# Weight parts made two units ahead, in pieces: a four-layer network on one core

## The chip, the cores and the metric

One core of a Trainium2 chip runs the whole network in one launch. The metric is the device time of that launch in microseconds (us). The five engines of the core run on their own and meet at semaphores: TensorE (PE, matrix products into PSUM), VectorE (DVE), ScalarE (ACT), GpSimd (POOL) and SyncE (SP, which here only issues DMA).

## The reference, cut to what matters

Three of the four layers are of this kind; the input is 4 x 32 x 32 x 16, and each layer is added to its input after a group norm (8 groups of 2 channels, over a whole image):

```python
first   = einsum('ijyx,byxc->bijc', M, inputs)
kern    = G as (h*w*f) filters of 3 x 3 x c          # one filter for each (i, j, f)
shifted = conv(inputs, kern)                         # b, (h w f), y, x
diff    = relu(inputs[:, None, None] - shifted)
second  = einsum('ijyx,bijyxc->bijc', W, diff)
out     = first - second
```

For each of the 1024 x 16 filters a full 32 x 32 image is made, clamped, weighted and summed to one number per batch. The third layer is another thing: running maxima and minima over intervals, then two steps of `max over k of sigmoid(ft[i, k] + rt[k, j] + b)`.

The convolution's 144 taps and channels are the contraction. The kernel takes `relu(x - s)` as `-min(s - x, 0)` by taking 1 off the filter's middle tap (`pick`), and keeps near float32 accuracy by splitting weights and input into an upper part (12 mantissa bits masked off) and the rest, and summing products of the parts.

## The kernel before

The work is cut into 6 phases (3 convolution layers, 2 halves of the batch), 8 tiles of 128 filters' places, and 32 steps per tile: 16 output channels `f` times 2 batches `b`. That makes 1536 steps. Four `f` are a unit: 192 units of eight steps, and each unit's weights are loaded and made ready once.

A unit's weights come as `raw` (slots 0, 1: the first 128 rows; slot 2: the last 16 rows repeated). `prep` takes the picked 1 off slot 1. `prep_rest` makes the four parts that the matmuls read:

```python
    RAWS = 3
    ...
    def prep(u, at=0, to=FU, eng=nc.gpsimd):
        ...
        eng.tensor_tensor(raws[u][:, 1, at:to], raws[u][:, 1, at:to], pick[...], ALU.subtract)   # L174

    def prep_rest(u, at=0, to=FU, eng=nc.gpsimd):
        ...
        high = upper(w8, f"w{u}{at}")                                  # VectorE, L164
        nc.scalar.activation(WD, high, AF.Copy, scale=-EPS)            # ScalarE, L197
        halve(W9, w9, low_w)                                           # ScalarE, L142
        eng.tensor_copy(WU, high)                                      # GpSimd,  L199
        eng.tensor_tensor(WL, w8, high, ALU.subtract)                  # GpSimd,  L200
        for r in (slice(32, 64), slice(96, 128)):
            eng.tensor_tensor(W9[r], W9.bitcast(F32)[r], w9[r], ALU.add)      # GpSimd, L202
        eng.tensor_tensor(WD, WD.bitcast(F32), WL.bitcast(F32), ALU.add)      # GpSimd, L203
```

Each of the parts has two buffers (`wpool`, bufs=2). A step has two halves, and the second half of one step is issued behind the first half of the next:

```python
    def first_part(step):
        ps = bank_pair(...)                       # one of 4 pairs of PSUM banks
        products(ps, WU x iy (2 slots), WL x iz (2 slots))             # TensorE, 8 matmuls
        nc.scalar.activation(ps, ps, AF.Copy, scale=1.0 + EPS)         # ScalarE, L531
        return ps

    def second_part(step, ps):
        products(ps, WD x iyz (2 slots), W9 x im9)                     # TensorE, 6 matmuls
        nc.vector.scalar_tensor_tensor(junk, ps, 0.0, chunks[n], op0=ALU.min, op1=ALU.mult,
                                       accum_out=accs[...])            # VectorE, L545

    def conv_layer(phase, behind):
        for t in range(NT):
            ...
            for at, (f, b) in enumerate(steps):
                u = n * NU + f // FU
                if at % (FU * GB) == 1:           # once per unit
                    prep_rest(u + 1)
                    prep(u + 2)
                    load_raw(u + 3)
                if at == 4:
                    load_chunk(n + 1)
                step = (phase, t, f, b)
                open_steps.append((step, first_part(step)))
                if len(open_steps) > 1:
                    second_part(*open_steps.pop(0))
                wait -= 1
                if wait <= 0:
                    wait = next(behind, 1 << 20)  # a piece of the next phase's work
```

`behind` is a generator. It gives out the work that the next phase needs (group norm, the input written to DRAM and read back shifted, its split into `iy`, `iz`, `iyz`, the interval layer, the products with `M`) piece by piece; `yield 5` means that five steps pass until the next piece. Two parts of it matter here:

```python
    def group_norm(g, name, dst):
        part = sums(X[g], ...)                        # VectorE
        yield 2
        m = mean_of(part, ...)                        # GpSimd partition_all_reduce, L240
        yield 5
        ... mean, xc                                  # VectorE
        yield 1
        ... squares, part                             # VectorE
        yield 2
        v = mean_of(part, ...)                        # GpSimd partition_all_reduce, L240
        yield 5
        nc.scalar.activation(rstd, v, AF.Sqrt, ...)   # ScalarE
        yield 2
        ...
    def before_conv(g, layer):
        yield from group_norm(...)
        nc.vector.transpose(xt[g]..., xn)
        ... write xt to DRAM (xs), four DMA on the ScalarE and SyncE queues
        yield 2
        ... read it back as 9 shifted copies (raw), 24 DMA on the ScalarE and SyncE queues
        yield 9
        for b in range(GB):
            split(nc.gpsimd, g, b, ...)
            yield 3
        ...
```

The interval layer holds its tables in a buffer of 8192 float32 per partition (`tables`), which is the buffer of the `M` matrix at other times (tag `big`), and has two further buffers for the sums (`dp`).

At the start, the input of batch 0 is normalized on ScalarE and VectorE, and that of batch 1 on GpSimd, behind the first step.

Of the kernel before, what the change touches and what calls it, by code (L numbers as in the profile page):

```python
# [8 lines left out]
F32 = mybir.dt.float32  # L9
F32R = mybir.dt.float32r  # L10
I32 = mybir.dt.int32
AF = mybir.ActivationFunctionType
ALU = mybir.AluOpType
AX = mybir.AxisListType

P = 128
B, H, C = 4, 32, 16
NG = 2
GB = B // NG
GC = GB * C  # L20
# [9 lines left out]
FU = 4  # L30
# [4 lines left out]
T1 = H + 1  # L35
# [5 lines left out]
def net_kernel(ctx: ExitStack, tc: tile.TileContext, x, xq, xi, convs, iv_w, iv_b, out):  # L41
# [19 lines left out]
    nc = tc.nc  # L61
# [3 lines left out]
    wpool = ctx.enter_context(tc.tile_pool(name="wpool", bufs=2))  # L65
    work = ctx.enter_context(tc.tile_pool(name="work", bufs=1))
    ivp = ctx.enter_context(tc.tile_pool(name="ivp", bufs=1))
# [16 lines left out]
    nc.sync.dma_start(XQ, xq)  # L84


    RAWS = 3
    raws, units, chunks = {}, {}, {}

    def load_raw(u):  # L90
        if u < n_chunks * NU:
            n = u // NU
            raws[u] = wpool.tile([P, 3, FU, P], F32, tag="raw", bufs=RAWS, name=f"raw_{u}")
            nc.sync.dma_start(raws[u], convs[phases[n // NT][1]][2][n % NT, u % NU])
# [18 lines left out]
    F0 = 2  # L113
    raws[0] = wpool.tile([P, 3, FU, P], F32, tag="raw", bufs=RAWS, name="raw_0")
    nc.scalar.dma_start(raws[0][:, :, :F0], convs[0][2][0, 0][:, :, :F0])
# [25 lines left out]
    def halve(dst, src, mask):  # L141
        nc.scalar.activation(dst, src, AF.Copy, scale=mask[:, 1:2])  # L142
# [16 lines left out]
    def upper(src, name):  # L159

        t = work.tile([P, 2, PITCH], F32, tag="upper", bufs=2, name=f"upper_{name}")
        t = t.rearrange("p s n -> p (s n)")[:, : src.shape[1] * src.shape[2]]
        t = t.rearrange("p (s n) -> p s n", s=src.shape[1])
        nc.vector.tensor_scalar(  # L164
            t.bitcast(I32), src.bitcast(I32), HIGH, None, op0=ALU.bitwise_and
        )
        return t

    def prep(u, at=0, to=FU, eng=nc.gpsimd):

        if u >= n_chunks * NU:
            return
        f0 = u % NU * FU
        eng.tensor_tensor(  # L174
            raws[u][:, 1, at:to], raws[u][:, 1, at:to],
            pick[:, f0 + at : f0 + to].unsqueeze(2).to_broadcast([P, to - at, P]),
            ALU.subtract,
        )

    def prep_rest(u, at=0, to=FU, eng=nc.gpsimd):  # L180

        if u >= n_chunks * NU:
            return
        if at == 0:
            units[u] = [
                wpool.tile([P, 2, FU, P], F32R, tag=tag, name=f"{tag}_{u}")
                for tag in ("WU", "WL", "WD")
            ] + [wpool.tile([P, FU, P], F32R, tag="W9", name=f"W9_{u}")]
        src = raws[u]
        if to == FU:  # L190
            del raws[u]
        w8 = src[:, :2, at:to].rearrange("p s f k -> p s (f k)")
        w9 = src[:, 2, at:to]
        WU, WL, WD = (t[:, :, at:to].rearrange("p s f k -> p s (f k)") for t in units[u][:3])
        W9 = units[u][3][:, at:to]
        high = upper(w8, f"w{u}{at}")
        nc.scalar.activation(WD, high, AF.Copy, scale=-EPS)  # L197
        halve(W9, w9, low_w)
        eng.tensor_copy(WU, high)  # L199
        eng.tensor_tensor(WL, w8, high, ALU.subtract)  # L200
        for r in (slice(32, 64), slice(96, 128)):
            eng.tensor_tensor(W9[r], W9.bitcast(F32)[r], w9[r], ALU.add)  # L202
        eng.tensor_tensor(WD, WD.bitcast(F32), WL.bitcast(F32), ALU.add)  # L203

    def split(eng, g, b, name):

        high = upper(raw[:, :2, b], f"x{name}{b}")
        eng.tensor_copy(iy[g][:, :, b], high)
        eng.tensor_tensor(iz[g][:, :, b], raw[:, :2, b], high, ALU.subtract)

    def scale_low(g, b):
        z = iz[g][:, :, b]
        nc.scalar.activation(z, z.bitcast(F32), AF.Copy, scale=1.0 / EPS)  # L213

    def difference(eng, g, b):
        eng.tensor_tensor(  # L216
            iyz[g][:, :, b], iy[g].bitcast(F32)[:, :, b], iz[g].bitcast(F32)[:, :, b], ALU.subtract
        )
# [152 lines left out]
    def interval_layer(g):  # L371

        R = 2 * GC
# [4 lines left out]
        tables = big.tile([P, 8192], F32, tag="big", name=f"tables_{g}")  # L378
        n = (H + M) * (M + H)
# [19 lines left out]
        k = 0  # L399
# [10 lines left out]
            )  # L410
            yield 2

        r = tables[: R + GC, 2 * n : 2 * n + T1 * T1].rearrange("p (i j) -> p i j", j=T1)
        nc.gpsimd.memset(r[:R], 0.0)
        nc.gpsimd.affine_select(
            out=r[:R, :H, 1:], in_=pp[k][:, :H, M:], pattern=upper, compare_op=ALU.is_ge, fill=0.0,
# [35 lines left out]
        def step(name, ftp, rt, bias):  # L452

            ft = ivp.tile([P, QI, T1], F32, tag="ft", name=f"ft_{name}{g}")
            nc.scalar.copy(ft, ftp)  # L455
            yield 2
            s = ivp.tile([P, QI, T1], F32, tag="s", name=f"s_{name}{g}")
            last = None
            for i in range(QI + 1):
                if i < QI:  # L460
                    t = ivp.tile([P, T1, T1], F32, tag="dp", bufs=2, name=f"dp_{name}{g}{i}")
                    nc.gpsimd.tensor_tensor(  # L462
                        t,
                        ft[:, i, :].unsqueeze(1).to_broadcast([P, T1, T1]),
                        rt,
                        ALU.add,
                    )
                if last is not None:
                    nc.vector.tensor_reduce(s[:, i - 1, :], last, axis=AX.X, op=ALU.max)
                last = t  # L470
                yield 6
            for q in range(NQ):
                o = slice(GC * q, GC * (q + 1))
                nc.scalar.activation(
                    r[R:, QI * q : QI * (q + 1), :], s[o], AF.Sigmoid, bias=bias[o]
                )
            yield 2
# [82 lines left out]
    def conv_layer(phase, behind):  # L560


        wait = 0
        accs[phase] = work.tile([P, NT, GC], F32, tag="acc", bufs=2, name=f"acc_{phase}")
        for t in range(NT):
            n = phase * NT + t
            steps = [(f, b) for f in range(C) for b in range(GB)]
            if n == 0:
                steps.sort(key=lambda s: (s[0] // FU, s[1]))
            for at, (f, b) in enumerate(steps):  # L570
                u = n * NU + f // FU
                if at % (FU * GB) == 1:
                    prep_rest(u + 1)
                    prep(u + 2)
                    load_raw(u + 3)
                if at == 4:
                    load_chunk(n + 1)
                step = (phase, t, f, b)
# [5 lines that stand above are left out]
                    wait = next(behind, 1 << 20)  # L584
        for _ in behind:
            pass
# [96 lines left out]
    def sides(eng, b, slot):  # L683

        v = raw[:, slot, b].rearrange("p (y x) -> p y x", x=HP)
        if slot == 2:
            eng.memset(v[:, :, H - 1 : H], 0.0)
            eng.memset(v[64:, HI - 1, :H], 0.0)
        for side, at in (
            ("left", v[:, :, 0]), ("right", v[:, :, H - 1]),  # L690
            ("top", v[:, 0, :H]), ("bottom", v[:, HI - 1, :H]),
        ):
            if f"{side}{slot}" in keep:
                eng.tensor_scalar_mul(at, at, keep[f"{side}{slot}"])

    def normal(eng, b, slot):
        v = raw[:, slot, b, :RUN]
        if eng is nc.scalar:
            eng.activation(v, v, AF.Identity, bias=minus_mean0[:, b : b + 1])
            eng.activation(v, v, AF.Copy, scale=rstd0[:, b : b + 1])  # L700
        else:
            eng.tensor_scalar(  # L702
                v, v, mean0[:, b : b + 1], rstd0[:, b : b + 1], op0=ALU.subtract, op1=ALU.mult
            )
# [10 lines left out]
    difference(nc.vector, 0, 0)  # L715
    halve_rest(im9[0][:, 0], raw[:, 2, 0], low_x)
    load_raw(1)
    load_raw(2)
    prep(0, F0, FU, nc.vector)
    prep_rest(0, F0, FU)  # L720
    prep(1)

    def rest_of_start():

        nc.sync.dma_start(X[0], x[0])
        for slot in (0, 1, 2):
            normal(nc.gpsimd, 1, slot)
            sides(nc.gpsimd, 1, slot)
        yield 1
        split(nc.vector, 0, 1, "00")  # L730
        scale_low(0, 1)
        difference(nc.vector, 0, 1)
        yield 1
        halve(im9[0][:, 1], raw[:, 2, 1], low_x)
        halve_rest(im9[0][:, 1], raw[:, 2, 1], low_x)
        nc.gpsimd.memset(zero, 0.0)
        zeros(0)
        xns[0] = work.tile([P, NT, GC], F32, tag="xn", bufs=2, name="xn_00")
        yield from group_norm(0, "c00", xns[0])
# [79 lines left out]
```

## Time and profile before

Two runs took 3530.45 and 3538.63 us, median 3534.54. The profiled execution spans 3538.9 us.

| operation, by line | engine | count | mean of one |
|---|---|---|---|
| matmul 64 x 512 | TensorE | 21504 | 428 to 442 ns, two at a time |
| scaling of PSUM, L531 | ScalarE | 1536 | 1002 ns |
| min, times, sum, L545 | VectorE | 1536 | 1223 ns |
| `WD`, L197 | ScalarE | 193 | 1053 ns |
| `W9` halved, L142 | ScalarE | 193 | 704 ns |
| `upper_w`, L164 | VectorE | 193 | 722 ns |
| `WU`, L199 | GpSimd | 192 | 1038 ns |
| `WL`, L200 | GpSimd | 192 | 2378 ns |
| `W9` sum, L202 | GpSimd | 384 | 1278 ns |
| `WD` sum, L203 | GpSimd | 192 | 2396 ns |
| `prep`, L174 | GpSimd | 191 | 1091 ns |

How to read it: TensorE works through steps in order, and all else is there to keep it fed. The matmuls of two halves of the array run together, so the mean of one is about twice the time between starts. The page lists each group with its busy time and the idle time of its engine just before it, and names who ended that idle time. The chain of waits follows the end of the program back from each instruction to what released it. The 40 slices of the page show TensorE at 7 or 8 tenths nearly everywhere after the start, and the granted clock between 8 and 9 tenths: the time is spread over the whole span, not sitting in one place.

### The profile page before, as it was taken

How to read it: one execution, taken by the hardware profiler on the slowest of the kernel's cores; microseconds unless marked ns; L12 is line 12 of the kernel's file. 1: busy time of each engine (PE TensorE's matmuls, PEld its weight loads, DVE VectorE, ACT ScalarE, POOL GpSimd, SP SyncE). 2: the span in 40 equal slices, each digit the busy share in tenths (PEclk: the TensorE clock that was granted, in tenths of full speed). 3: DMA queues.
4: the chain of work that ended last, by engine and by line, in shares of the span. 5: the costliest groups of instructions: out<-in, count | busy, mean ns of one | idle time of the engine just before them, and what ended most of it. 6: DMA issues, size and time to landing. Idle time of an engine off the chain costs nothing.

```text
span 3538.9 us, 56292 instructions
## 1 busy us (share of the span) xinstructions
PE 2966.8 (84%) x21970; PEld 2346.7 (66%) x21970; DVE 2155.1 (61%) x3519; ACT 1874.1 (53%) x1993; POOL 1983.0 (56%) x1284
## 2 busy tenths in 40 slices
PE   5788888788888778888878888787888878888888
PEld 4566777566676666777656667565676656777767
DVE  5565666566666556666656666666666655656666
ACT  4454555455555545555544555454555554555555
POOL 4564555465555464555556665565666555555554
PEclk8899999899999989999988899898889989999999
DMA  2221111211111131111111111221111122111110
GB/s 89 72 99 49 56 56 51 63 57 51 51 57 60 43 116 46 59 59 51 53 46 52 52 42 51 63 66 42 43 51 51 51 79 90 51 52 57 57 55 11
DMA packets 49514, 203.78 MB, mean 58 GB/s; under 512 B 11872, under 2 KB 13280, under 8 KB 48480
## 3 DMA queue, kind: packets, MB, share of 16 engines
q1 hardware_dynamic: 42688, 195.07, 16.4%
q10 hardware_dynamic: 6432, 5.10, 0.7%
q8 instruction: 173, 2.83, 0.3%
q14 instruction: 93, 0.76, 0.1%
q0 software_dynamic: 128, 0.02, 0.0%
HBM read 199.19 MB, written 0.98 MB: 57 GB/s over the span
## 4 chain that ended last, share of the span: by engine, by line
PE 73%; ACT 9%; issue 6%; POOL 5%; DVE 4%; DMA 2%; ACTq 0%; DVEq 0%; POOLq 0%; SPq 0%
PE pc L510 73%; ACT pc L531 5%; ACT W L142 4%; DVE junk L545 2%; POOL W L202 1%; DMA raw<-xs 1%; POOL WD L203 1%; POOL WL L200 1%; DVE upper_w L164 1%; PE pf L318 1%; POOL raw L174 0%; DMA xs<-xt 0%; POOL tables L384 0%; POOL raw L702 0%; POOL WU L199 0%
## 5 line engine op out<-in xcount | busy, mean ns | idle before, releaser
L545 DVE SCALAR_TENSOR_TENSOR junk<-pc,WT 128x1024 f32<-128x1024 f32 x1536 | 1878.9, 1223 | 1328.8 <-PE pc L510 1284.9
L531 ACT ACTIVATE pc<-pc 128x1024 f32<-128x1024 f32 x1536 | 1527.9, 1002 | 1174.3 <-PE pc L510 1128.0
L510 PE MATMUL pc<-iyz,WD 64*128 64x512 f32 x6144 | 1134.6, 442 | 531.4 <-ACT pc L531 519.1
L510 PEld LDWEIGHTS pc<-iyz,WD 64*128 64x128 f32 x6144 | 657.1, 206 | 755.8 <-ACT pc L531 558.5
L510 PE MATMUL pc<-iy,WU 64*128 64x512 f32 x6144 | 1103.1, 431 | 18.3 <-DVE junk L545 10.0
L510 PE MATMUL pc<-iz,WL 64*128 64x512 f32 x6144 | 1096.2, 428 | 8.5 <-POOL WL L200 7.3
L199 POOL CAST WU<-upper_w 128x1024 fp32r<-128x1024 f32 (+1 forms) x192 | 199.4, 1038 | 1220.5 <-DVE upper_w L164 1183.4
L510 PEld LDWEIGHTS pc<-iy,WU 64*128 64x128 f32 x6144 | 676.9, 205 | 178.1 <-DVE junk L545 14.8
L510 PEld LDWEIGHTS pc<-iz,WL 64*128 64x128 f32 x6144 | 677.0, 203 | 153.8 <-POOL WL L200 9.3
L510 PE MATMUL pc<-im,W 64*128 64x512 f32 x3072 | 695.9, 433 | 0.0
L200 POOL TENSOR_TENSOR WL<-raw,upper_w 128x1024 fp32r<-128x1024 f32 (+1 forms) x192 | 456.6, 2378 | 115.1 <-PE pc L510 57.2
L202 POOL TENSOR_TENSOR W<-W,raw 32x512 fp32r<-32x512 f32 (+1 forms) x384 | 490.8, 1278 | 26.4
L203 POOL TENSOR_TENSOR WD<-WD,WL 128x1024 fp32r<-128x1024 f32 (+1 forms) x192 | 460.0, 2396 | 15.0
L197 ACT ACTIVATE WD<-upper_w 128x1024 fp32r<-128x1024 f32 (+1 forms) x193 | 203.2, 1053 | 395.4 <-DVE upper_w L164 384.2
L510 PEld LDWEIGHTS pc<-im,W 64*128 64x128 f32 x3072 | 341.3, 206 | 74.9
L174 POOL TENSOR_TENSOR raw<-raw,pick 128x512 f32<-128x512 f32 x191 | 208.3, 1091 | 0.0
L164 DVE TENSOR_SCALAR upper_w<-raw 128x1024 int32<-128x1024 int32 (+1 forms) x193 | 139.4, 722 | 19.7 <-POOL raw L174 19.3
L142 ACT ACTIVATE W<-raw,low_w 128x512 fp32r<-128x512 f32 (+1 forms) x193 | 135.9, 704 | 0.0
L545 DVE DVE_READ_ACCUMULATOR junk<-pc,WT 128x1 f32 x1536 | 127.4, 83 | 0.0
L462 POOL TENSOR_TENSOR dp_b<-ft_b,rt_r 128x1089 f32<-128x1089 f32 x16 | 37.4, 2342 | 19.2 <-ACT ft_b L455 19.2
L462 POOL TENSOR_TENSOR dp_a<-ft_a,rt_r 128x1089 f32<-128x1089 f32 x16 | 37.3, 2342 | 0.0
L216 POOL TENSOR_TENSOR iyz<-iy,iz 128x1088 fp32r<-128x1088 f32 x10 | 25.3, 2532 | 9.9 <-ACT iz L213 9.9
(119 smaller groups left out, 361.3 us busy)
## 6 DMA issues: line engine op xcount, KB each, us to landing
raw<-in_g SPq DMA_DIRECT2D x191, 768.0 KB, 4.3
WT<-in_w SPq DMA_DIRECT2D x48, 512.0 KB, 3.5
MT<-in_mt SPq DMA_DIRECT2D x6, 2048.0 KB, 12.0
raw<-xs ACTq DMA_DIRECT2D x60, 67.8 KB, 3.2
raw<-xs SPq DMA_DIRECT2D x60, 67.8 KB, 3.2
raw<-in_xi SPq DMA_DIRECT2D x3, 271.0 KB, 4.3
raw<-in_xi SPq DMA_DIRECT2D x1, 813.0 KB, 7.4
raw<-in_g ACTq DMA_DIRECT2D x1, 384.0 KB, 4.6
```

What stands on the lines that cost most here:

```text
L142: nc.scalar.activation(dst, src, AF.Copy, scale=mask[:, 1:2])
L164: nc.vector.tensor_scalar(t.bitcast(I32), src.bitcast(I32), HIGH, None, op0=ALU.bitwise_and)
L174: eng.tensor_tensor(raws[u][:, 1, at:to], raws[u][:, 1, at:to], pick[:, f0 + at : f0 + to].unsqueeze(2).to_broadcast([P, to - at, P]), ALU ...
L197: nc.scalar.activation(WD, high, AF.Copy, scale=-EPS)
L199: eng.tensor_copy(WU, high)
L200: eng.tensor_tensor(WL, w8, high, ALU.subtract)
L202: eng.tensor_tensor(W9[r], W9.bitcast(F32)[r], w9[r], ALU.add)
L203: eng.tensor_tensor(WD, WD.bitcast(F32), WL.bitcast(F32), ALU.add)
L462: nc.gpsimd.tensor_tensor(t, ft[:, i, :].unsqueeze(1).to_broadcast([P, T1, T1]), rt, ALU.add,)
L510: nc.tensor.matmul(ps[:, h, :], lhsT=w[r], rhs=v.rearrange("p (y x) -> p y x", x=HP)[r, :, :H], start=first and k == 0, stop=k == len(pair ...
L531: nc.scalar.activation(ps, ps, AF.Copy, scale=1.0 + EPS)
L545: nc.vector.scalar_tensor_tensor(junk, ps.rearrange("p h n -> p (h n)"), 0.0, chunks[n], op0=ALU.min, op1=ALU.mult, accum_out=accs[phase][ ...
```

## The change

What it does:

1. Weights are made ready two units ahead instead of one (`AHEAD`), so `WU`, `WL`, `WD`, `W9` have three buffers; `raw` has two instead of three.
2. `prep_rest` becomes a generator. Its pieces are issued ahead of steps 0 (`upper_w`), 2 (`WD`, `WL`), 4 (`WU`, the `WD` sum), 5 (`W9` halved) and 6 (the `W9` sums) of a unit, and not all at step 1. `prep` is issued at step 7 for the unit whose `upper_w` comes at the next step.
3. The copy `WU` moves from GpSimd to ScalarE.
4. The interval layer's sums `dp` lie in the rest of the tables' buffer. This frees the space for the third set of weights.
5. Batch 1 of the first input is normalized on VectorE; unit 1's weights are issued after that.

What it is for: no engine should have a block of weight work in front of what TensorE waits for.

```diff
-    RAWS = 3
+    RAWS = 2
+    AHEAD = 2
...
-    def prep_rest(u, at=0, to=FU, eng=nc.gpsimd):
+    def prep_parts(u, at=0, to=FU, eng=nc.gpsimd):
...
-                wpool.tile([P, 2, FU, P], F32R, tag=tag, name=f"{tag}_{u}")
+                wpool.tile([P, 2, FU, P], F32R, tag=tag, bufs=AHEAD + 1, name=f"{tag}_{u}")
...
         high = upper(w8, f"w{u}{at}")
+        yield
         nc.scalar.activation(WD, high, AF.Copy, scale=-EPS)
+        eng.tensor_tensor(WL, w8, high, ALU.subtract)
+        yield
+        nc.scalar.copy(WU, high)
+        eng.tensor_tensor(WD, WD.bitcast(F32), WL.bitcast(F32), ALU.add)
+        yield
         halve(W9, w9, low_w)
-        eng.tensor_copy(WU, high)
-        eng.tensor_tensor(WL, w8, high, ALU.subtract)
+        yield
         for r in (slice(32, 64), slice(96, 128)):
             eng.tensor_tensor(W9[r], W9.bitcast(F32)[r], w9[r], ALU.add)
-        eng.tensor_tensor(WD, WD.bitcast(F32), WL.bitcast(F32), ALU.add)
+
+    def prep_rest(u, at=0, to=FU, eng=nc.gpsimd):
+        for _ in prep_parts(u, at, to, eng):
+            pass
...
-        r = tables[: R + GC, 2 * n : 2 * n + T1 * T1].rearrange("p (i j) -> p i j", j=T1)
+        r, *dp = (
+            tables[:k, 2 * n + i * T1 * T1 : 2 * n + (i + 1) * T1 * T1].rearrange(
+                "p (i j) -> p i j", j=T1
+            )
+            for i, k in enumerate((R + GC, P, P))
+        )
...
-                    t = ivp.tile([P, T1, T1], F32, tag="dp", bufs=2, name=f"dp_{name}{g}{i}")
+                    t = dp[i % 2]
...
-                if at % (FU * GB) == 1:
-                    prep_rest(u + 1)
-                    prep(u + 2)
-                    load_raw(u + 3)
+                k = at % (FU * GB) - (3 if u == 0 else 0)
+                if k == 0:
+                    parts = prep_parts(u + AHEAD)
+                    next(parts, None)
+                elif k in (2, 4, 5, 6):
+                    next(parts, None)
+                if k == 2:
+                    load_raw(u + AHEAD + 1)
+                if at % (FU * GB) == 7:
+                    for _ in parts:
+                        pass
+                    prep(u + AHEAD + 1)
...
     load_raw(1)
-    load_raw(2)
     prep(0, F0, FU, nc.vector)
     prep_rest(0, F0, FU)
-    prep(1)
 
     def rest_of_start():
 
         nc.sync.dma_start(X[0], x[0])
         for slot in (0, 1, 2):
-            normal(nc.gpsimd, 1, slot)
-            sides(nc.gpsimd, 1, slot)
-        yield 1
+            normal(nc.vector, 1, slot)
+            sides(nc.vector, 1, slot)
         split(nc.vector, 0, 1, "00")
+        load_raw(2)
+        prep(1)
+        prep_rest(1)
+        prep(2)
         scale_low(0, 1)
         difference(nc.vector, 0, 1)
         yield 1
```

More of the change, by code (lines that the diff above doesn't have):

```diff
@@ L185, in prep_rest @@
             units[u] = [
-                wpool.tile([P, 2, FU, P], F32R, tag=tag, name=f"{tag}_{u}")
+                wpool.tile([P, 2, FU, P], F32R, tag=tag, bufs=AHEAD + 1, name=f"{tag}_{u}")
                 for tag in ("WU", "WL", "WD")
-            ] + [wpool.tile([P, FU, P], F32R, tag="W9", name=f"W9_{u}")]
+            ] + [wpool.tile([P, FU, P], F32R, tag="W9", bufs=AHEAD + 1, name=f"W9_{u}")]
         src = raws[u]
```

## The prediction

> **What bounds the kernel now.** The page first. TensorE is busy 84% of the span, far more than any other engine, and what ends its idle time is in the costliest groups: the second part of a step (the matmuls on `WD`) waits for ScalarE's scaling of PSUM at L531.
>
> ```profile
> PE 2966.8 (84%) x21970; PEld 2346.7 (66%) x21970; DVE 2155.1 (61%) x3519; ACT 1874.1 (53%) x1993; POOL 1983.0 (56%) x1284
> ...
> L510 PE MATMUL pc<-iyz,WD 64*128 64x512 f32 x6144 | 1134.6, 442 | 531.4 <-ACT pc L531 519.1
> ...
> L199 POOL CAST WU<-upper_w 128x1024 fp32r<-128x1024 f32 (+1 forms) x192 | 199.4, 1038 | 1220.5 <-DVE upper_w L164 1183.4
> ```
>
> Then the waits say how often: 208 times, against 192 units of weights. So it is a thing of the unit, not of the step.
>
> ```profile
> PE pc L510 <- ACT pc L531: 519.1, 208, 8.5
> ```
>
> Then the chain of waits over one unit. It leaves TensorE once per unit, and goes through the halving of `W9` (L142) and one scaling:
>
> ```profile
> 1004.78 0.24 issue
> 1005.01 0.71 ACT W L142
> 1005.72 0.92 ACT pc L531
> 1006.64 0.04 issue
> 1006.68 15.38 PE pc L510 x112
> 1022.07 0.02 issue
> ```
>
> In the timeline of ScalarE around it, the preparation of the next unit stands in one block ahead of the scaling: 1.72 us of waiting for VectorE's `upper_w`, 1.06 us for `WD`, 0.71 us for `W9`.
>
> ```profile
> 1004.05 1.06 ACT L197 ACTIVATE WD<-upper_w 128x1024 fp32r<-128x1024 f32 x1 [1.72 <-DVE upper_w L164]
> 1005.01 0.71 ACT L142 ACTIVATE W<-raw,low_w 128x512 fp32r<-128x512 f32 x1
> 1005.63 1.91 ACT L531 ACTIVATE pc<-pc 128x1024 f32<-128x1024 f32 x2
> ```
>
> Last, the windows of 2 us (columns: the stretch and its length, busy time of TensorE, weight loads, VectorE, ScalarE, GpSimd, then the granted clock, DMA share, GB/s): the granted clock falls to half after the gap, for some 3 us.
>
> ```profile
> 1004.00:1006.00 2.00, 0.72 (x6) 0.27 (x3) 1.10 (x2) 1.95 (x3) 1.91 (x2) 1.00 0.00 0
> ...
> 1008.00:1010.00 2.00, 2.00 (x12) 1.61 (x10) 1.23 (x2) 0.06 (x1) 1.94 (x2) 0.50 0.00 0
> ...
> 1014.00:1016.00 2.00, 2.00 (x20) 1.58 (x18) 1.23 (x2) 1.30 (x2) 0.00 (x0) 1.00 0.00 0
> ```
>
> An undisturbed step: the `WD` matmuls start at 1011.66, 1013.37, 1015.07, 1016.77, 1018.48 and 1020.18 in TensorE's timeline, 8.52 us for 5 steps, 1.704 us each, and TensorE has no gap in them. Eight such steps are 13.64 us. In the chain, TensorE restarts at 904.89 and, 11 units on, at 1092.39: 17.05 us per unit. So each unit loses 3.4 us: 2.0 us of gap and the rest of half clock.
>
> [...]twice per all-reduce: 5.76 us ahead of it and 7.05 to 7.15 us ahead of the next tensor_tensor, and 32 MODIFY_POOL_CONFIG entries for 16 all-reduces.
>
> ```profile
> 664.11 0.44 POOL L240 PARTITION_ALL_REDUCE sum_vc<-part_vc  x1 [5.76 <-issue]
> 664.45 1.10 POOL L199 CAST WU<-upper_w 128x1024 fp32r<-128x1024 f32 x1
> 672.60 2.38 POOL L200 TENSOR_TENSOR WL<-raw,upper_w 128x1024 fp32r<-128x1024 f32 x1 [7.05 <-ACT pc L531]
> ```
>
> **The change, part by part.**
>
> *Pieces.* ScalarE's three pieces now stand ahead of steps 2 (`WD`), 4 (`WU`) and 5 (`W9`), `upper_w` being issued on VectorE two steps before the first. A scaling lasts 1.01 us and comes every 1.704, so ScalarE is free for 0.70 us per step. A piece of 1.06 us, taking 0.96 us of the queue, makes one scaling about 0.2 us late (1.88 instead of 1.70 after the one before). TensorE starts the second part 1.50 us after a scaling's start (1011.87 to 1013.37), so 0.45 us of lateness is free. `WU` then `W9` in neighbouring steps add up to under 0.3 us late. The trace has the trial: at 719.74 a lone ScalarE piece of 1.20 us stands between two scalings, and TensorE runs through it.
>
> ```profile
> 718.82 1.01 ACT L531 ACTIVATE pc<-pc 128x1024 f32<-128x1024 f32 x1 [0.65 <-PE pc L510]
> 719.74 1.20 ACT L142 ACTIVATE im<-raw,low_x 128x1088 fp32r<-128x1088 f32 x1
> 720.84 1.02 ACT L531 ACTIVATE pc<-pc 128x1024 f32<-128x1024 f32 x1
> 722.23 1.01 ACT L531 ACTIVATE pc<-pc 128x1024 f32<-128x1024 f32 x1 [0.38 <-PE pc L510]
> ```
>
> So I take the unit's stall to vanish whole. Loads per 13.64 us unit: ScalarE 8 x 0.96 + 0.96 + 0.96 + 0.65 = 10.3; VectorE 8 x 1.23 + 0.72 = 10.6; GpSimd, without the cast, 2.38 + 2.40 + 2 x 1.28 + 1.09 = 8.4. None passes TensorE.
>
> *What becomes tight.* Before, `prep` (L174) came eight steps ahead of the `upper_w` that reads it; now one step. Counted from a unit's start, the scaling of step 4 ends at 4 x 1.70 + 0.97 + 0.3 + 1.0 = 9.1, the halving at 9.8, the two `W9` adds at 12.4, `prep` at 13.4. VectorE comes to `upper_w` at 13.64 + 1.23 = 14.9, and `WD` on ScalarE (as well as the four PSUM buffers) bears it up to 3.1 us after the unit's start, 16.7. So GpSimd may be 3.3 us late at no cost, and beyond that TensorE waits.
>
> *Group norms.* There are 8, each with two all-reduces eight steps apart, one per unit. Each puts 5.9 + 0.44 + 7.1 = 13.4 us into GpSimd's queue. Two units with one each need 2 x (13.4 + 8.4 + 0.2 of small gaps) = 44 us where 27.3 are there and 3.3 may be owed: 13.4 us of stall. 8 x 13.4 = 107 us.
>
> *What stays.* Five times ScalarE sits behind its own DMA issues (`raw<-xs`, 44.3 us in all): TensorE's gaps there were 7 to 8.5 us; 5 x 8 = 40. In each of the two interval layers, ten max passes of 16.0 us in all (18.1 + 13.9 over two) fall on VectorE within 20 steps, where it has 34.1 - 24.6 - 1.7 = 7.8 us: 8 us over; and ScalarE waits about 8 us for the transposed tables (8.43 in the trace). 2 x 16 = 32. Other matmuls (`pf` 21.3, the interval's 12.4): 34.
>
> *Start and end.* Batch 1 on VectorE costs 3 x 0.56 + some 1.6 instead of GpSimd's 10.4 us (25.94 to 36.3). But `WD`, `WU`, `W9` of unit 1 now stand ahead of the second scaling, with `upper_w` at about 26, so steps flow from about 32 us instead of 39. By 32 TensorE has done 3.7 us of work: 28 lost, and 3 of half clock; 4.4 from the last matmul to the end: 35.
>
> *The M matrix's buffer, and RAWS at 2.* The sums (`dp`) move in behind `r` in the same buffer, to pay for a third set of weights. They are still two, so nothing new is waited for. A raw buffer is loaded at step 2 and read at 12.4 us, and landing takes 4.3 us. No time in either.
>
> *Sum.* 1536 x 1.704 = 2617; + 34 other matmuls + 35 ends + 107 + 40 + 32; about 25 gaps of half clock at 1.7 = 43; 20 for splits of the input and sums that meet a late GpSimd. 2928, so 2930 us.
>
> **Rivals.** (1) *The wait moves to `prep`.* If GpSimd's `prep` is in truth some 2 us beyond its margin in every unit, VectorE stands before `upper_w` and 192 x 2 = 384 us stay: 3310. For it: the one-step distance. Against: 3.3 us of margin, and 5.0 us idle per unit. (2) *Small stalls thrice a unit.* If a piece costs 0.3 us of TensorE each time, 192 x 3 x 0.3 = 173: 3100. Against it: the lone piece at 719.74. (3) *The clock.* If 0.911 is a ceiling of long work and not the result of gaps, the floor is 2617 / 0.911 = 2873, and the total about 3140. Against: 1.00 in each window with a full TensorE. (4) *Better than told.* If the group norms' lateness is absorbed by weights made two units ahead, 107 + 27 of half clock go: 2795. Against: `upper_w` blocks VectorE, whatever is ready.
>
> **Range and chances.** The floor plus the sure terms (2617 + 34 + 35 + 40) is 2726, so below 2800 little may stall. 3060 allows half of rival 1 or most of rival 2. 2810 to 3060 should hold it 8 times in 10. Under 3464 is faster by 2%: even rival 1 is. 0.96 faster, 0.03 within, 0.01 slower.
>
> **What would show it.** Right: TensorE's wait for L531 in some 30 places instead of 208; steps of 1.70 us through whole units; the granted clock near 0.98; the gaps left at the group norms, released through `upper_w` behind `prep` on GpSimd. Wrong: VectorE's `upper_w` waiting for `prep` in most units (rival 1), a gap of a few tenths after each ScalarE piece (2), a clock under 1.00 in gapless stretches (3).

## The result, and the profile after

| | before | after |
|---|---|---|
| time, median of two runs | 3534.54 us | 3008.43 us (3003.81 to 3013.04) |
| profiled span | 3538.9 us | 3002.1 us |
| TensorE idle in the span | 572 us | 254 us |
| its gaps over 0.3 us | 232, 567 us | 68, 247 us |
| of these over 1.7 us | 201 | 40 |
| mean granted clock | 0.911 | 0.960 |

The ratio is 0.8512, with a 95% interval of 0.8441 to 0.8582: the change takes off 526 us. It does so in two parts of one cause. TensorE's gaps fell by 320 us; and the work lost to a halved clock, summed as busy time times (1 - clock) over windows of 1 us, fell from 271 to 71 us.

The page of the kernel after, busy time and the 40 slices of TensorE and its clock:

```profile
PE 2748.5 (92%) x21970; PEld 2153.5 (72%) x21970; DVE 2218.9 (74%) x3529; ACT 2037.2 (68%) x2186; POOL 1800.0 (60%) x1081
...
PE   4679999879999969999989999798999979999999
...
PEclk8889999989999989999999999798999989999999
```

TensorE's row now reads 9 nearly everywhere; behind the start, a 6, 7 or 8 marks a place with a group norm, DMA issues or the splits behind them, or several of these. The waits of the kernel after, in the order of the answer (engine and line, who ended it, us in total, times, the longest):

```profile
DVE upper_w L165 <- POOL raw L175: 175.9, 35, 16.1
PE pc L524 <- DVE junk L559: 163.6, 45, 13.7
...
PE pc L524 <- ACT pc L545: 66.7, 26, 8.2
```

The wait for the scaling of PSUM (L531 before, L545 now) was 519.1 us in 208 places; it is 66.7 us in 26. The larger wait is a new one: for VectorE to free PSUM (163.6 us), and the line above it says why VectorE was late: it stood before `upper_w`, which waited for `prep` on GpSimd.

A plain unit, ScalarE's timeline of the kernel after (start, duration, and in brackets the wait ahead):

```profile
828.86 1.01 ACT L545 ACTIVATE pc<-pc 128x1024 f32<-128x1024 f32 x1 [0.69 <-PE pc L524]
829.78 1.05 ACT L199 ACTIVATE WD<-upper_w 128x1024 fp32r<-128x1024 f32 x1
830.73 1.02 ACT L545 ACTIVATE pc<-pc 128x1024 f32<-128x1024 f32 x1
832.26 1.01 ACT L545 ACTIVATE pc<-pc 128x1024 f32<-128x1024 f32 x1 [0.52 <-PE pc L524]
833.18 1.04 ACT L202 CAST WU<-upper_w 128x1024 fp32r<-128x1024 f32 x1
834.12 1.02 ACT L545 ACTIVATE pc<-pc 128x1024 f32<-128x1024 f32 x1
835.07 0.71 ACT L143 ACTIVATE W<-raw,low_w 128x512 fp32r<-128x512 f32 x1
835.67 1.02 ACT L545 ACTIVATE pc<-pc 128x1024 f32<-128x1024 f32 x1
837.38 1.01 ACT L545 ACTIVATE pc<-pc 128x1024 f32<-128x1024 f32 x1 [0.69 <-PE pc L524]
```

Each piece lies between two scalings, in the 0.7 us that ScalarE had waited for TensorE, and the next scaling but one waits for TensorE again: the delay is gone within two or three steps. TensorE has no gap in this stretch. VectorE starts `upper_w` at 827.39 and again at 841.02: the unit takes 13.63 us, where it took 17.05.

A group norm, GpSimd's timeline of the kernel after:

```profile
1041.19 0.44 POOL L249 PARTITION_ALL_REDUCE sum_mc<-part_mc  x1 [6.17 <-ACT pc L545]
1048.65 2.34 POOL L203 TENSOR_TENSOR WD<-WD,WL 128x1024 fp32r<-128x1024 f32 x1 [7.01 <-issue]
1051.07 2.59 POOL L208 TENSOR_TENSOR W<-W,raw 32x512 fp32r<-32x512 f32 x2
1053.73 1.04 POOL L175 TENSOR_TENSOR raw<-raw,pick 128x512 f32<-128x512 f32 x1
```

VectorE's and TensorE's, at the same group norm's two sums:

```profile
1054.80 0.69 DVE L165 TENSOR_SCALAR upper_w<-raw 128x1024 int32<-128x1024 int32 x1 [8.71 <-POOL raw L175]
```

```profile
1079.23 1.22 PE L524 MATMUL pc<-iy,WU 64*128 64x512 f32 x4 [7.10 <-DVE junk L559]
1080.25 1.06 PE L524 MATMUL pc<-iz,WL 64*128 64x512 f32 x4
...
1083.87 0.65 PE L524 MATMUL pc<-iyz,WD 64*128 64x512 f32 x4
```

An all-reduce of 0.44 us costs 6.17 us ahead of it and 7.01 us behind it. `prep` stands in line behind, `upper_w` behind `prep`, the freeing of PSUM behind `upper_w`, and TensorE 7.10 us behind all of them. Then four matmuls take 1.22 and 1.06 us instead of 0.65: the halved clock (0.50 granted from 1080 to 1082 us), on top of the gap. The 22 matmuls from 1079.23 to 1083.87 take 4.64 us; at 1.704 us for 14 they would take 2.68.

### The profile page after: what moved, and what is told of

Same layout as the page of the kernel before. It is cut to its first block, busy times and chain, and to the rows that moved or that the text cites. A ratio compares the mean times of both kernels' runs of the same rounds, so it can differ in the third digit from the quotient of the medians.

```text
span 3002.1 us, 56056 instructions
## 1 busy us (share of the span) xinstructions
PE 2748.5 (92%) x21970; PEld 2153.5 (72%) x21970; DVE 2218.9 (74%) x3529; ACT 2037.2 (68%) x2186; POOL 1800.0 (60%) x1081
## 5 line engine op out<-in xcount | busy, mean ns | idle before, releaser
L545 ACT ACTIVATE pc<-pc 128x1024 f32<-128x1024 f32 x1536 | 1550.0, 1010 | 729.2 <-PE pc L524 705.5
L524 PE MATMUL pc<-iy,WU 64*128 64x512 f32 x6144 | 1045.8, 416 | 172.1 <-DVE junk L559 163.6
L524 PE MATMUL pc<-iyz,WD 64*128 64x512 f32 x6144 | 1037.5, 413 | 66.8 <-ACT pc L545 66.7
L524 PE MATMUL pc<-iz,WL 64*128 64x512 f32 x6144 | 1033.9, 412 | 1.0 <-ACT iz L222 1.0
L524 PEld LDWEIGHTS pc<-iy,WU 64*128 64x128 f32 x6144 | 610.7, 193 | 355.6 <-DVE junk L559 195.7
L524 PEld LDWEIGHTS pc<-iyz,WD 64*128 64x128 f32 x6144 | 614.2, 193 | 232.1 <-ACT pc L545 76.8
L524 PEld LDWEIGHTS pc<-iz,WL 64*128 64x128 f32 x6144 | 618.7, 193 | 156.3 <-ACT iz L222 1.7
L524 PE MATMUL pc<-im,W 64*128 64x512 f32 x3072 | 646.7, 410 | 0.0
L203 POOL TENSOR_TENSOR WD<-WD,WL 128x1024 fp32r<-128x1024 f32 (+1 forms) x192 | 461.4, 2403 | 133.1 <-ACT WD L199 65.8
L165 DVE TENSOR_SCALAR upper_w<-raw 128x1024 int32<-128x1024 int32 (+1 forms) x193 | 147.2, 763 | 176.0 <-POOL raw L175 175.9
L202 ACT CAST WU<-upper_w 128x1024 fp32r<-128x1024 f32 (+1 forms) x193 | 200.2, 1037 | 29.3 <-DMA raw<-xs 19.8
L569 DVE TENSOR_TENSOR X<-X,acc 128x32 f32<-128x32 f32 x48 | 62.8, 1308 | 1.7
L476 POOL TENSOR_TENSOR tables<-ft_a,rt_r 128x1089 f32<-128x1089 f32 x16 | 37.5, 2345 | 0.3
```

The costliest lines, as they stand in the source:

```text
L165: nc.vector.tensor_scalar(t.bitcast(I32), src.bitcast(I32), HIGH, None, op0=ALU.bitwise_and)
L202: nc.scalar.copy(WU, high)
L476: nc.gpsimd.tensor_tensor(t, ft[:, i, :].unsqueeze(1).to_broadcast([P, T1, T1]), rt, ALU.add,)
L524: nc.tensor.matmul(ps[:, h, :], lhsT=w[r], rhs=v.rearrange("p (y x) -> p y x", x=HP)[r, :, :H], start=first and k == 0, stop=k == len(pair ...
```

## The experiments

Theory: the gain is the spreading. A piece that fits ScalarE's slack costs TensorE nothing, a block costs a gap per unit and half clock after it; the lead of two units brings nothing of its own; what is left is group norms and DMA issues. Rivals: the lead of two does the work (E1, E2); a deeper pipeline would have done as well (E6); the moved copy does it (E3). Each time below is a median with its range, each ratio is to the kernel before, with its 95% interval. The diffs are against the kernel after, but for E6. The kernel after has two runs, and its interval reaches 25 us to either side: differences against it of 66 or 71 us are known no closer than that, and those of 10 us not at all.

**E1, one unit ahead, in pieces.** Two sets of weights instead of three; the start issues its unit's weights accordingly.

```diff
-    AHEAD = 2
+    AHEAD = 1
```

> The changed kernel, pieces spread as they are, but weights made one unit ahead (two buffers). Theory (the block ahead of the scaling was the cost, and spreading is what removes it): the last part of a unit, the W9 sums, is done about 12.4 us after the unit before it starts, and is read only at about 15, so steady units stay without a gap; 2990 to 3060 us. Late GpSimd work after an all-reduce now shows as TensorE waiting for WL, WD or W9 on GpSimd instead of for VectorE. Rival (the second unit of lead is what removes the wait): the unit's gap comes back in most units, 3200 us or more.

Measured: 2999.44 us (2997.9 to 3000.75), ratio 0.8461 (0.8447 to 0.8475). This is the whole gain, with a lead of one; the kernel after lies within its own interval of it. TensorE's wait for VectorE fell to 65.8 us, and waits for GpSimd's own products came in its place: 35.6 us for the `WD` sum, 14.8 for `WL`, 13.1 for the `W9` sum. At a group norm the work is late with either lead; mainly the name of the one waited for differs. The four waits add up to 129 us, 34 less than the 163.6, of which little shows in the time: TensorE has 101 gaps over 0.3 us instead of 68 and loses 79 us instead of 71 to half clock, and the rest is open. So no worth of the lead of two shows in this kernel.

**E2, two units ahead, in one block.** The three sets of weights stay, but all pieces stand ahead of step 0, in the order of the kernel before, and `WU` is on GpSimd again.

```diff
         high = upper(w8, f"w{u}{at}")
-        yield
         nc.scalar.activation(WD, high, AF.Copy, scale=-EPS)
-        eng.tensor_tensor(WL, w8, high, ALU.subtract)
-        yield
-        nc.scalar.copy(WU, high)
...
-        yield
         halve(W9, w9, low_w)
-        yield
+        eng.tensor_copy(WU, high)
+        eng.tensor_tensor(WL, w8, high, ALU.subtract)
...
```

> The changed kernel, weights two units ahead, but all pieces of a unit issued in one block ahead of its first step, in the order of the kernel before and with WU on GpSimd. Theory: the block stands ahead of a scaling again, with the wait for upper_w in it: about 200 waits of TensorE for the scaling, 3.4 us per unit or a little more, 3550 to 3700 us. Rival (lead): nobody needs these weights for two units, so about 3010 to 3050 us.

Measured: 3569.89 us (3565.7 to 3574.09), ratio 1.0072 (1.005 to 1.0094). The whole gain is gone, and the old wait is back in the waits of this kernel:

```profile
PE pc L521 <- ACT pc L542: 595.3, 205, 14.1
```

E1 and E2 together settle the first rival: lead without pieces gives nothing, pieces without lead give all.

**E12, one block, without the wait for VectorE.** `upper_w` is issued ahead of step 0 as in the kernel after; `WD`, `WU` and `W9` follow in one block ahead of step 2. It asks which half of the block hurt: its length, or ScalarE's wait for `upper_w` in front of it (1.72 us before).

```diff
-                elif k in (2, 4, 5, 6):
-                    next(parts, None)
+                elif k == 2:
+                    for _ in parts:
+                        pass
```

> The changed kernel with upper_w in its place, two steps ahead, but WD, WU and W9 in one block ahead of step 2: the block without the wait for VectorE. ScalarE then has 0.96 + 0.96 + 0.61 = 2.5 us between two scalings; the later one starts some 3.45 us after the earlier instead of 1.70, 1.75 late, of which 0.45 is free. Theory: a gap of about 1.3 us in nearly each of the 192 units, 250 us; whether the clock falls with so short a gap is open: 3260 us if it stays, up to 3500 us if every gap costs what it did in the kernel before. Rival (only the wait for upper_w made the block harmful): about 3010 us.

Measured: 3215.91 us (3214.1 to 3217.84), ratio 0.9078 (0.9065 to 0.9092). In a plain unit, ScalarE and TensorE of this kernel:

```profile
818.79 1.05 ACT L199 ACTIVATE WD<-upper_w 128x1024 fp32r<-128x1024 f32 x1
819.73 1.04 ACT L202 CAST WU<-upper_w 128x1024 fp32r<-128x1024 f32 x1
820.67 0.73 ACT L143 ACTIVATE W<-raw,low_w 128x512 fp32r<-128x512 f32 x1
821.30 1.92 ACT L545 ACTIVATE pc<-pc 128x1024 f32<-128x1024 f32 x2
```

```profile
822.37 0.75 PE L524 MATMUL pc<-iyz,WD 64*128 64x512 f32 x4 [1.14 <-ACT pc L545]
837.39 0.75 PE L524 MATMUL pc<-iyz,WD 64*128 64x512 f32 x4 [1.14 <-ACT pc L545]
```

A unit takes 15.02 us: 1.4 us more than with lone pieces, 2.0 less than before. The block is longer than before (`WU` is in it), yet the gap is 1.14 us and not 2.0, for the wait for `upper_w` is gone; and after 1.14 us the matmuls start at full clock (0.75 us for four, not 1.02 or 1.22). So of the 3.4 us per unit that the kernel before lost, the block's bare length makes 1.4 us even with one more piece in it; ScalarE's wait for VectorE brought the gap to 2.0 us, and with it the halved clock.

**E6, the kernel before with three steps open.** The pieces stay in one block, but a scaling may be a step later.

```diff
-                if len(open_steps) > 1:
+                if len(open_steps) > 2:
...
-    second_part(*open_steps.pop(0))
+    while open_steps:
+        second_part(*open_steps.pop(0))
```

The `pf` sums of the interval layer are taken one group at a time, and the next phase's pieces start two steps later, so that banks and data suffice.

> The kernel before, with three steps open instead of two: a step's second part is issued behind the first parts of the next two steps (and the two products with M one after the other). The weight block is left as it is. Theory (the block is longer than what one open step bears): TensorE has 1.70 us more to do before it needs the late scaling, of a gap of 2.0 us some 0.3 is left and the clock stays up in most units: 192 x 3 us less, 2950 to 3100 us. Rival (the four PSUM buffers and VectorE become the limit, since a buffer is now needed again 1.7 us after its sum may start): the gap moves to TensorE waiting for VectorE's L545 and the time stays above 3300 us.

Measured: 3183.02 us (3182.39 to 3183.65), ratio 0.8981 (0.8963 to 0.8999): between the two expectations, and neither. Two thirds of the gain come without spreading anything.

```profile
PE pc L508 <- DVE junk L543: 154.8, 127, 11.2
...
PE pc L508 <- ACT pc L529: 127.7, 176, 10.6
```

Of the 176 waits for ScalarE, 157 are of 0.3 us, as the theory had it, and the mean clock is 0.960. But TensorE now waits 154.8 us in 127 places for VectorE to free PSUM, as three of the four pairs of banks are held by open steps. 42 of these waits, 47 us, come right behind an add of VectorE at the end of a tile that takes some 2.4 us instead of 0.19 (the last section has what they overlap). Depth hides a block by using up the slack of the buffers behind it.

**E3, `WU` on GpSimd again**, and nothing else.

```diff
-        nc.scalar.copy(WU, high)
+        eng.tensor_copy(WU, high)
```

> The changed kernel with the copy WU back on GpSimd, in the same place. Theory (spreading is what counts, and GpSimd has room): steady units stay without a gap, as prep ends 1.04 us later and VectorE then waits under a microsecond, which four PSUM buffers bear; at the group norms, splits and the interval layer GpSimd is later by another 1 us per unit, some 20 to 30 us in all: 3030 us, between 3010 and 3060. Rival (the move of WU to ScalarE is a main part of the gain): prep misses its margin in every unit, 3100 us or more.

Measured: 3022.71 us (3021.68 to 3026.84), ratio 0.8539 (0.8513 to 0.8565). By the medians the moved copy is worth some 14 us, by the ratios some 10; the intervals overlap, so a gain from it is not shown, and it is at most a small part of the 526 us. The wait of `upper_w` for `prep` is 192.5 us instead of 175.9, in 29 places instead of 35, which fits a GpSimd that comes out of a group norm later with more in its queue.

**E10, batch 1 normalized on GpSimd again.**

```diff
-            normal(nc.vector, 1, slot)
-            sides(nc.vector, 1, slot)
+            normal(nc.gpsimd, 1, slot)
+            sides(nc.gpsimd, 1, slot)
```

> The changed kernel with batch 1 of the first input normalized on GpSimd again, ahead of unit 1's weights. Theory (prediction, start): GpSimd takes some 10 us for it before prep of unit 1, upper_w of unit 1 and the block behind it; the second scaling is some 7 to 10 us later, steps flow from about 42 us instead of 34: 3015 us, between 3008 and 3022. Rival (the start is hidden behind other waits): no difference.

Measured: 3017.01 us (3015.79 to 3021.18), ratio 0.8521 (0.8505 to 0.8536). As a difference of times, 9 us, this cannot be told, for the intervals overlap. The trace tells it: TensorE's last gap of the start is 16.17 us and ends at 40.87; in the kernel after it is 8.22 us and ends at 33.95. Some 7 to 8 us, once.

**E4, the sums over partitions on TensorE.** The 16 all-reduces become products with a matrix of ones into a PSUM bank.

```diff
-            m = work.tile([P, GC // 2], F32, tag="sum", name=f"sum_{name}")
-            nc.gpsimd.partition_all_reduce(m, part, channels=P, reduce_op=bass_isa.ReduceOp.add)
+            m = bank(f"sum_{name}")[:, : GC // 2]
+            nc.tensor.matmul(m, lhsT=ones, rhs=part, start=True, stop=True)
...
-        yield 5
+        yield 1
```

> The changed kernel with the 16 cross-partition sums of the group norms made by a TensorE product with a matrix of ones instead of GpSimd's all-reduce; the result is read from PSUM one step later. Theory ([...]prep late, upper_w late): the 16 gaps at the group norms, 123 us in the changed kernel, go, and with them some 2.5 us of half clock each, 40 us: 2845 us, between 2815 and 2890; no MODIFY_POOL_CONFIG is left, VectorE's wait for prep falls from 176 us to under 30. Rival (the gaps come from the group norm's own work on VectorE and ScalarE): 2970 us or more, with gaps of 5 to 7 us left in the same places.

Measured: 2872.54 us (2863.94 to 2875.33), ratio 0.8101 (0.8085 to 0.8116). 136 us less than the kernel after. No gap over 1.6 us is left at a group norm, and MODIFY_POOL_CONFIG stands in this trace at the start alone (in the kernel after, each all-reduce has two such entries ahead of it and two behind, 64 for the 16; the kernel before has as many, and not the 32 of the prediction). TensorE's wait for VectorE goes from 163.6 to 47.4 us, that of `upper_w` for `prep` from 175.9 to 31.9 (a little above the 30 expected), and the clock from 0.960 to 0.982.

**E5, `prep` ahead of the `W9` sums in GpSimd's queue.** The order of GpSimd's queue alone is changed.

```diff
+                if u and k == 5:
+                    prep(u + AHEAD + 1)
...
-                    prep(u + AHEAD + 1)
+                    if u == 0:
+                        prep(u + AHEAD + 1)
```

> The changed kernel with prep issued ahead of the W9 sums instead of behind them; nothing else. Theory (the one-step distance from prep to upper_w is where a late GpSimd reaches VectorE): prep ends some 5 us earlier in a steady unit, so GpSimd may be some 8 us late instead of 3.3; each group norm's stall is some 5 us shorter and the gaps of 3 to 4 us at the splits go: 8 x 5 + 15 and a few half clocks, 60 us less, 2950 us, between 2920 and 2980. Rival (the order inside GpSimd's queue doesn't matter, since the loads are due to GpSimd's sum of work): 2990 us or more.

Measured: 2942.23 us (2940.61 to 2945.11), ratio 0.8314 (0.8292 to 0.8335). 66 us for the place of one instruction. `prep` is what VectorE, and so TensorE, waits for; the `W9` sums (2.6 us) are not needed for another unit. The wait of `upper_w` halves in number (35 to 17), and TensorE's for VectorE falls to 106.6 us.

**E8, the DMA of the input all on SyncE's queue.** The reads are issued four per step, and not 24 at once.

```diff
-                (nc.scalar, nc.sync)[at % 2].dma_start(
+                nc.sync.dma_start(
...
+                if at % 4 == 0:
+                    yield 1
```

> The changed kernel with the DMA of the input (xs written, raw read back) all issued by SyncE, four reads per step, none by ScalarE. Theory (ScalarE sits behind its own DMA issues): the ten gaps at the five places, 46 us in the changed kernel, and their half clock go: 60 us less, 2945 us, between 2915 and 2975. Rival ([...]the raw weights' loads now stand behind these DMA, prep is late, and VectorE waits instead): 2990 us or more, with VectorE's wait for prep grown.

Measured: 2937.27 us (2933.31 to 2942.12), ratio 0.8299 (0.8276 to 0.8322). TensorE's wait for ScalarE falls from 66.7 to 20.6 us, while `upper_w` waits for `prep` as before (174.7 us). The 71 us are accounted for: TensorE's idle time falls from 254 to 204 us, and the work lost to half clock from 71 to 52.

**E9, E4, E5 and E8 together.**

> Sums by TensorE, prep ahead of the W9 sums, and DMA on SyncE together, to see whether the causes add up. From the 2872 us measured with TensorE's sums: less 46 us of gaps and 18 of half clock at the DMA, less 15 to 20 at the splits: 2790 us, between 2760 and 2825. If the three share a cause, or one makes another worse (loads behind DMA on SyncE, prep waiting for a load), it stays above 2840 us.

Measured: **2778.32 us** (2774.66 to 2781.35), ratio 0.7849 (0.7828 to 0.787). It beats both kernels: 756 us less than the kernel before, 230 less than the one after. The three alone bring 136 + 66 + 71 = 273 us; E4 and E5 mend the same wait, so sharing part of it is to be expected. The page and the waits of this kernel:

```profile
PE 2701.8 (97%) x22002; PEld 2137.1 (77%) x22002; DVE 2228.5 (80%) x3529; ACT 2034.4 (73%) x2186; POOL 1793.3 (65%) x1066
```

```profile
PE pc L528 <- DVE junk L563: 33.6, 44, 1.5
...
PE pc L528 <- ACT pc L549: 19.7, 11, 8.1
...
DVE upper_w L165 <- POOL raw L175: 7.3, 5, 1.8
```

The clock is 0.995. TensorE is bound by its own matmuls: its gaps are 69 us, 25 of them at the start.

**E11, E9 with a lead of one.** `AHEAD = 1` as in E1. If the lead was worth nothing only because the other waits hid it, it should show here.

> Sums by TensorE, prep ahead of the W9 sums, DMA on SyncE, with the weights one unit ahead. If the lead of two units is worth nothing once GpSimd isn't late (as one ahead gave 2999 against 3008 us in the changed kernel), 2778 us within 15. If the lead hid rests of lateness at the splits and in the interval layer, TensorE waits for WL, WD and W9 there: 2800 us or more.

Measured: 2798.92 us (2797.09 to 2810.62), ratio 0.7908 (0.7889 to 0.7928), against 0.7849 (0.7828 to 0.787). The lead is worth 20 us once nothing else stands in front of it; the waits show 21.8 us of TensorE for the `W9` sum. So the verdict of E1 holds for the kernel it was taken in, and not for this one.

## Why the prediction was right

Predicted 2930, measured 3008, inside the range of 2810 to 3060. Term by term:

| term | predicted, us | measured, us |
|---|---|---|
| stall of each unit | 0 | 0 in plain units (13.63 us each) |
| start, until steps flow | 28 | 25 |
| group norms | 107 | about 123 in 16 gaps |
| DMA issues on ScalarE | 40 | 46 in ten gaps |
| interval layers | 32 | about 20 |
| splits, and products with `M` | 20 | about 32 |
| half clock | 3 + 43 | 71 |

- *Pieces in the slack: right.* The lone pieces cost nothing. `WU`, reckoned at the 1.06 us of a `WD`, takes 1.04 on ScalarE. `prep` ends at 839.67, 1.35 us before `upper_w`; the working had it 1.5 us before. Rival 1 (the wait moves to `prep` in every unit) shows in 35 places only: 16 of them, 146 of the 175.9 us, at the group norms, the rest at the start, the splits and the interval layers; rival 2 (three small stalls per unit) in no plain unit.
- *The clock follows the gaps: right.* Rival 3 (0.911 as a ceiling) falls: 0.960 here and 0.995 in E9, with more work per us in each. "1.00 in each window with a full TensorE" does not hold right behind a gap: the prediction's own window of 1008 to 1010 us has a full TensorE at 0.50.
- *The lead of two units: right.* It had no term of its own, and rival 4 was given little for the reason that VectorE stands at `upper_w` whatever is ready. E1 shows the worth is nothing, and E11 under which condition it is not.
- *The start, and the M matrix's buffer at no cost.* Steps flow from 33.95 us, predicted about 32, and E10 shows that batch 1 on VectorE is what moved them. The buffer has no experiment of its own; no wait for `dp` or for `raw`'s buffers stands among the waits of TensorE.
- *Mis-sized: the half clock.* The step was "about 25 gaps of half clock at 1.7 = 43", besides 3 for the start, and a clock near 0.98. 1.7 us is what one stretch of 3.41 us at half clock costs a full TensorE, and 124 of the 152 stretches of the kernel before were of that length. Here the clock was 0.960, and 71 us were lost in 32 stretches of half clock, 2.2 us each: both factors were too small. Sixteen gaps at the group norms were reckoned (rival 4 gives them 27 us of half clock) and came, but at more than 1.7. Of the ten gaps at the DMA, nine are over 1.7 us, where five places were reckoned. Six more stretches, 12 us, come from the splits, where the sum names no half clock.
- *Mis-sized: the gaps,* by 23 us in sum (254 us of idle time, 231 in the terms with the 4 of the end). At the group norms, the 12 gaps behind the first phase are 6.65 us each, where the term has 6.7; the four of the first phase make 42.9 us. There is more at the splits and less in the interval layers.
- *The DMA term: near in size, one cause missing.* The working has ScalarE behind its own issues, once per place. Each place has two gaps. The second, of 5.3 to 8.0 us, is that. Ahead of the first, of 1.2 to 3.4 us, ScalarE's issue of the write to `xs` waits for VectorE's `xt` (at four of the five places ScalarE stood 4.7 to 10.4 us at it), and the scalings wait behind it.
- *Not in the sum:* 2617 + 34 of matmuls, 254 of idle time and 71 of half clock make 2976 of the 3002 us of the span. Some 26 us are left. Part of it is the restart: the first four matmuls after a gap take 0.75 us even at full clock (31 gaps of the kernel after, 0.75 to 0.77), and 0.65 in a flow. In a flow two start 3 ns apart, the next two 0.24 us behind them, and each lasts some 0.405 us (1014.10 to 1014.83 before), 1.7 times the time between pairs ("about twice" in the reading of the profile before). In one phase a tile without any gap took 55.04 us where others took 54.51, for no reason that the trace names. The rest is open. With the 23 us of the gaps and the 25 of the half clock, these 26 us make up most of the 78 between 2930 and 3008.

## What to carry to other kernels

Cut the work that stands in one engine's queue with the critical operation into pieces no longer than that engine's slack, and issue each well behind its own inputs; that counts for more than a lead of whole units. Then look at what the next wait is made of: the place of one instruction in a queue (66 us), DMA issues on the engine that TensorE waits for (71 us), a 0.44 us all-reduce that costs 13 us around it (136 us for 16). Count gaps as well as their sum, for half clock mostly comes with the longer ones (in the two kernels, in or within 3.5 us behind 184 of 236 gaps over 1.9 us, and 3 of 37 of 1.0 to 1.9 us), and a lead that is worth nothing now may be worth something once the other waits are gone.

## What the hardware showed that was not expected

*When the clock halves.* In the traces of the kernels before and after, the granted clock is 1.00 or 0.50, and but for the last one, every stretch of either lasts a whole multiple of 3.41 us (303 stretches before, 65 after). Cut into pieces of 3.41 us on these borders, called windows here, the two traces give, for a window at full clock, by TensorE's idle time in it:

| idle in the window, us | next window at full clock | next window at half clock |
|---|---|---|
| under 1.4 | 1398 | 0 |
| 1.4 to 1.9 | 65 | 18 |
| over 1.9 | 0 | 165 |

So in these two kernels about half a window of idle time was enough, and it mattered where a gap fell. Of 101 gaps of 1.9 to 2.1 us that stand alone (none over 0.3 us in the 12 us before, none in the 5 us after), 66 have 1.8 us or more within one window, and all of these were followed by a halved window; the other 35 are cut by the border of two windows, and none was. The kernel before had a gap of 2.0 us in nearly every unit, so its half clock came in many units and not in all: 199 gaps over 1.9 us, and 152 stretches of half clock. A window at half clock was followed by full clock only where TensorE was idle for less than 0.65 us of it (183 of 184; with more, none of 70). E12's 168 gaps of 1.0 to 1.2 us cost little more than their length, 1.4 us per unit; behind the one shown there, four matmuls take 0.75 us, as behind a gap at full clock.

*An add that takes seven times as long.* The line of the page of the kernel after:

```profile
L569 DVE TENSOR_TENSOR X<-X,acc 128x32 f32<-128x32 f32 x48 | 62.8, 1308 | 1.7
```

The same add had a mean of 248 ns before. In the trace of the kernel after, the five that overlap no GpSimd instruction take 0.19 us; of the other 43, 42 take 1.4 us and one 2.2, and 41 end 0.05 us after GpSimd's `WL` subtraction, the other two as long after its `iyz` sum; in E6, where they start with that subtraction, they take 2.4 us, and end 0.05 us after it too. In both, every add that overlaps such an instruction ends within 0.06 us of its end. In the kernel after it costs VectorE 51 us and TensorE nothing, as a tile with such an add still takes 32 steps of 1.703 us; in E6 it is behind 47 us of TensorE's waits.
